# A deformable-convolution, attention and expert kernel: three gifts of the last batch go to two chunks, and the last finish starts with three head groups

## The chip, the cores and the metric

The kernel runs on one core of one Trainium2 chip. The metric is the device time of one execution in microseconds (us). PE is TensorE, DVE is VectorE, ACT is ScalarE, POOL is GpSimd, and SP is SyncE, which issues nearly all DMAs.

## The reference

The input `x` is a batch of 4 images, 128 channels of 64 x 64 positions. Everything is in fp32.

```
x = x + deform_conv3x3(group_norm(x))            # 9 taps, bilinear samples, offsets and mask from a 3x3 conv
t = tokens(x)                                     # [4, 4096, 128]
u = layer_norm(t)
q = ring(cos(heads(u) + rx))                      # 16 heads of 8
s = softmax(q @ q.T / sqrt(8))                    # per head, 4096 x 4096, queries = keys = values
x1 = layer_norm(u + (s @ q) @ w_comb.T + b)
t = t + layer_norm(x1 + w2 @ relu(w1 @ (cos(x1[:8]) * cos(ry))))
t = t + top2_of_8_experts(layer_norm(t))          # router softmax, 8 products 128x128, two weighted sums
```

The scores of a head are the product of one matrix with itself, so the block of scores of keys c and queries d is the transpose of the block of keys d and queries c.

## The kernel before

The 4096 tokens of an image are 8 chunks of 512. The 16 heads are 4 groups of 4 (`NGRP`). A **run** is one chunk of queries `sc` with one head group `g` of one batch `b`. It walks over key tiles of 128 tokens, 32 of them, and each is one **step**: `scores` (L1253 and after) makes four products of 128 x 512 on PE and two exponentials of 128 x 1024 on ACT (L1270, tile `e`), and `context` (L1274 and after) multiplies these with the values and a column of ones on PE into one accumulator `acc` (L1281). So `acc` holds the weighted sums of the four heads and, for each head, the sum of the weights. At the end of the run DVE copies `acc` into `cu` (L1493), and `park_context` stores it in DRAM (`atd`).

**Gifts.** A chunk that has computed the exponentials of keys t and its own queries can turn them: DVE transposes them in 32 x 32 blocks into `st` (`turn`, L1140), SP stores 1 MB in DRAM (`etd`). A later chunk that owns the tokens t as queries then fetches this tile (`fetch`, L1195, tile `et`) and needs no scores and no exponentials for it; its PE only multiplies it with the values of the giver (`from_turned`, L1214, 32 small products a tile, in two halves). `gifts` says to whom chunk `sc` gives: to `sc + 1`. So in batch 3 chunks 1 to 7 each take 4 tiles and compute 28 steps instead of 32 in each run. Two fetch buffers (`NET = 2`, counted by `room`) and three turning buffers (`NST = 3`) exist. The fetches are asked for 5 steps before the run that takes them; SP issues a fetch when a buffer is granted, and `returned` passes it on.

**Order.** In the last batch, batch 3, the runs go chunk by chunk, four head groups each. Nothing is scheduled by the chip: the program writes out the order of all instructions of PE, DVE, SP and POOL. Between the instructions of two steps `Beside` puts work of other jobs: the preparation of the next batch (none in batch 3) and the **finishes**. `finish(b, ch)` takes the four stored contexts of a chunk, divides by the sums of weights (a reciprocal of `rd`, a round trip through DRAM that spreads it to 128 partitions, and a product at L901), and then does `attention_out`, `feed_forward` and `experts` for the 512 tokens, one dependent step after the other. At most two finishes are in work at once (`active`); others wait in `done`.

`Beside` keeps a model of time: each step is `STEP = 1.82` us, and each gives PE `RATE = 0.44` us of credit for other work. A job yields `need(pe, dve, lat, ...)` before it emits; its instructions are put into the order only where the model has credit and the engine is free. Products with taken tiles are such a job too (`turned`), before all others, with `pe=MM256` (0.44) for each half of a tile; what is left of it at a run's last step is emitted at once. After the last step `beside.drain()` emits all that is left.

Each engine executes its instructions in the order written out, and waits on semaphores for the others. SP's DMA issues are in the same written order.

Of the kernel before, what the change touches and what calls it, by code (L numbers as in the profile page):

```python
# [224 lines left out]
def kernel(  # L225
# [669 lines left out]
    def attention_out(b, ch, r, aT, a4):  # L895
# [4 lines left out]
        yield need(dve=ve(512), lat=0.2)  # L900
        nc.vector.tensor_tensor(aT, aT, a4.rearrange("p i c -> p (i c)"), ALU.mult)  # L901
        for i in range(4):
# [74 lines left out]
    def experts(b, ch, x4):  # L977
# [75 lines left out]
        for i in range(4):  # L1053
            ws = [temp2(f"eo{b}_{ch}_{i}_{hf}") for hf in range(2)]
            for hf in range(2):
                for part in range(2):
                    yield need(pe=MM256, dve=ve(512) if part else 0.0, lat=FREE, hold=not part)
                    if part == 0:
                        pe = misc(f"e_ps{b}_{ch}_{i}_{hf}")
                    e0 = 4 * hf + 2 * part  # L1060
                    by_columns(
                        pe[:, 256 * part : 256 * (part + 1)], uT[:, P * i : P * (i + 1)],
                        ew_sb[:, e0 : e0 + 2, :].rearrange("p e c -> p (e c)"), True, True,
                    )
                nc.vector.tensor_tensor(  # L1065
                    ws[hf], pe.rearrange("p (e c) -> p e c", c=C),
                    gt[:, i, 4 * hf : 4 * (hf + 1), None].to_broadcast([P, 4, C]), ALU.mult,
                )
            yield need(dve=ve(512))
# [13 lines left out]

    def finish(b, ch):
        x4 = temp2(f"x4_{b}_{ch}")
        nc.sync.dma_start(out=x4, in_=x2d[b][ch])

        rows = atd[b][ch].rearrange("g (h d) n -> (g h) d n", d=32)
        aT = temp2(f"aT{b}_{ch}", (P, CH))
        nc.sync.dma_start(out=aT, in_=rows[:, :HD])  # L1090
        rd = work.tile([P, CH // HD], F32, tag="rd", name=f"rd{b}_{ch}")
        nc.sync.dma_start(out=rd, in_=rows[:, HD].rearrange("h (q n) -> h q n", q=HD))
        r = temp2(f"r{b}_{ch}")
# [4 lines left out]
        yield need(lat=3.5)  # L1098
        nc.sync.dma_start(out=rdd[b][ch].rearrange("h q n -> (h q) n"), in_=rd)
        yield need(lat=6.0)  # L1100
        a4 = temp2(f"a4_{b}_{ch}")
        nc.sync.dma_start(
            out=a4.rearrange("p i c -> p (i c)"),
            in_=rdd[b][ch].rearrange("h q n -> h (q n)")[:, None, :].to_broadcast([HEADS, HD, CH]),
        )
# [3 lines left out]


    def park_context(b, g, sc, cu):
# [50 lines left out]

    room = [NET]
    asking = []

    def granted(emit):
        if room[0]:
            room[0] -= 1
            emit()
        else:  # L1170
            asking.append(emit)

    def returned():
        if asking:
            asking.pop(0)()
        else:
            room[0] += 1

# [21 lines left out]

    def from_turned(run, acc):

        for giver in takes[run]:
            qv = values.pop((run, giver)).rearrange("p t x -> p (t x)")
            for kt in range(4):
                while (run, giver, kt) not in fetched:
                    yield need(lat=1.0)
                e, landed = fetched.pop((run, giver, kt))
                for half in range(2):
                    yield need(pe=MM256, hold=None, after=landed)  # L1210
                    for t in (2 * half, 2 * half + 1):
                        for h in range(4):
# [6 lines left out]
                            )  # L1219
                returned()  # L1220

# [188 lines left out]
    with tc.manual_schedule(engines={PE, DVE, SP, POOL}):  # L1410
# [6 lines left out]
        while n < len(steps):  # L1417
# [48 lines left out]
            if following:  # L1466
                if following[0] != b and at == 0:
                    beside.drain("prepare")

                if at == 1:  # L1470
# [3 lines left out]
                if takes[run + 1] and at == len(ts) - 5:  # L1474
                    fetch_values(run + 1)
                    for giver in takes[run + 1]:
                        for kt in range(4):
                            granted(lambda a=(run + 1, giver, kt): fetch(*a))
            by_act = run < opening
# [95 lines left out]
```

## Time and profile before

| | |
|---|---|
| median of 3 runs | 7592.69 us (7573.33 to 7599.12) |
| the profiled execution | 7579.71 us, its span 7576.5 us |
| PE, ACT, DVE busy, share of the span | 94%, 91%, 59% |
| bytes moved by DMA | 1689.51 MB, mean 223 GB/s |
| batch 3, from the end of batch 2's last run to the copy of the last accumulator | 5812.3 to 7493.0 us |
| after that | 83.5 us |

The profile is one execution. A busy time is the sum of an engine's instructions, and PE's is modelled, since matmuls overlap. What a wait costs is seen in the stretch where it stands: an engine that waits for one that is never idle sets nothing.

### The profile page before, as it was taken

How to read it: one execution, taken by the hardware profiler on the slowest of the kernel's cores; microseconds unless marked ns; L12 is line 12 of the kernel's file. 1: busy time of each engine (PE TensorE's matmuls, PEld its weight loads, DVE VectorE, ACT ScalarE, POOL GpSimd, SP SyncE). 2: the span in 40 equal slices, each digit the busy share in tenths (PEclk: the TensorE clock that was granted, in tenths of full speed). 3: DMA queues.
4: the chain of work that ended last, by engine and by line, in shares of the span. 5: the costliest groups of instructions: out<-in, count | busy, mean ns of one | idle time of the engine just before them, and what ended most of it. 6: DMA issues, size and time to landing. Idle time of an engine off the chain costs nothing.

```text
span 7576.5 us, 180754 instructions
## 1 busy us (share of the span) xinstructions
PE 7113.9 (94%) x73848; PEld 2375.9 (31%) x73848; DVE 4465.9 (59%) x8950; ACT 6863.5 (91%) x7467; POOL 1653.2 (22%) x1326
## 2 busy tenths in 40 slices
PE   3688999899999999999999999999999999999997
PEld 2122222223333333333333323333333333333333
DVE  7755356667444877776544677775444554455434
ACT  0578999889999999999999998989999999999995
POOL 5544034443000433422000334431000000000000
PEclk6889999999999999999999999999999999999998
DMA  6777567978446878887655789897454466666661
GB/s 181 223 204 219 141 223 241 300 234 291 149 168 200 292 244 280 268 277 244 203 179 190 228 279 298 289 324 237 174 190 152 148 236 230 232 222 239 226 202 63
DMA packets 909788, 1689.51 MB, mean 223 GB/s; under 512 B 150754, under 2 KB 384124, under 8 KB 858268
## 3 DMA queue, kind: packets, MB, share of 16 engines
q1 hardware_dynamic: 809102, 1371.37, 54.9%
q0 software_dynamic: 92160, 302.06, 12.4%
q8 instruction: 579, 9.49, 0.5%
q10 hardware_dynamic: 7694, 4.52, 0.2%
q14 instruction: 253, 2.07, 0.1%
HBM read 1027.51 MB, written 650.14 MB: 221 GB/s over the span
## 4 chain that ended last, share of the span: by engine, by line
PE 80%; DMA 8%; DVE 4%; issue 2%; ACT 2%; SPq 1%; another core or an unknown queue 0%; POOL 0%; POOLq 0%; DVEq 0%; ACTq 0%
PE acc L1281 39%; PE sc L1261 24%; PE acc L1214 5%; PE e_ps L281 4%; PE conv_ps L281 3%; DMA et<-etd 2%; PE f_ps L281 2%; ACT e L1270 2%; DMA etd<-st 1%; DMA sT<-smd 1%; PE om_ps L533 1%; DMA smd<-tr 1%; DVE st L1140 1%; DVE v L645 1%; DMA cu<-part 1%
## 5 line engine op out<-in xcount | busy, mean ns | idle before, releaser
L1270 ACT ACTIVATE e<-sc 128x1024 f32<-128x1024 f32 x7400 | 6849.4, 1081 | 527.0 <-PE sc L1261 368.1
L1281 PE MATMUL acc<-e,qf 128*9 128x512 f32 (+1 forms) x29600 | 3938.3, 601 | 18.6 <-ACT cu L1491 7.5
L1261 PE MATMUL sc<-qT,kT 32*128 32x512 f32 x14800 | 2368.7, 499 | 153.3 <-ACT e L1270 84.8
L1261 PEld LDWEIGHTS sc<-qT,kT 32*128 32x128 f32 x14800 | 942.8, 183 | 3612.6 <-ACT e L1270 3130.4
L625 POOL DMA_INDIRECT v<-tab,idx x1152 | 1451.8, 1260 | 1579.3 <-DVE tr L686 956.2
L1140 DVE STREAM_TRANSPOSE st<-e 128x1024 f32<-128x1024 f32 x792 | 937.3, 1222 | 752.4 <-ACT e L1270 620.1
L1281 PEld LDWEIGHTS acc<-e,qf 128*9 128x9 f32 (+1 forms) x29600 | 682.4, 91 | 610.3 <-issue 346.8
L396 POOL TENSOR_TENSOR r<-ln_t,expo 128x4 f32<-128x4 f32 x96 | 112.2, 1169 | 3105.4 <-DVE ln_t L394 3057.0
L645 DVE TENSOR_TENSOR v<-v,wt 128x1536 f32<-128x1536 f32 x384 | 667.0, 1737 | 119.5 <-DMA v<-tab,idx 96.8
L1214 PE MATMUL acc<-et,qv 128*9 128x128 f32 x12672 | 506.4, 276 | 52.2 <-DMA et<-etd 44.6
L1065 DVE TENSOR_TENSOR eo<-e_ps,gt 128x512 f32<-128x512 f32 x256 | 175.2, 686 | 552.5 <-PE e_ps L281 547.5
L650 DVE TENSOR_TENSOR v<-v 128x768 f32<-128x768 f32 x384 | 367.2, 956 | 10.1
L281 PE MATMUL conv_ps<-sT,wconv_sb 128*32 128x256 f32 x4320 | 351.0, 399 | 15.7 <-DMA sT<-smd 11.6
L1214 PEld LDWEIGHTS acc<-et,qv 128*9 128x9 f32 x12672 | 270.0, 90 | 254.4 <-issue 212.6
L686 DVE STREAM_TRANSPOSE tr<-v 128x128 f32<-128x128 f32 x1080 | 249.4, 282 | 37.5 <-DMA etd<-st 28.7
L1493 DVE COPY cu<-acc 128x512 f32<-128x512 f32 x116 | 80.2, 692 | 306.3 <-PE acc L1281 260.8
L651 DVE TENSOR_TENSOR v<-v 128x384 f32<-128x384 f32 x384 | 215.7, 562 | 13.3
L396 POOL TENSOR_TENSOR rstd<-lt_t,expo 128x4 f32<-128x4 f32 x32 | 57.9, 1811 | 575.9 <-DVE lt_t L394 550.7
L281 PE MATMUL f_ps<-w_sb,h 128*32 128x128 f32 x4096 | 166.1, 282 | 0.1
L950 DVE TENSOR_SCALAR h<-h_ps,b_sb 128x512 f32<-128x512 f32 x128 | 94.9, 744 | 100.3 <-PE h_ps L948 89.9
L823 POOL COPY fx<-rn 128x512 f32<-128x512 f32 x32 | 26.8, 838 | 526.3 <-DVE rn L822 321.4
L965 DVE TENSOR_TENSOR a<-a,f_ps 128x512 f32<-128x512 f32 x32 | 21.9, 685 | 198.8 <-PE f_ps L281 198.8
(227 smaller groups left out, 3166.9 us busy)
## 6 DMA issues: line engine op xcount, KB each, us to landing
etd<-st SPq DMA_DIRECT2D x396, 1024.0 KB
et<-etd SPq DMA_DIRECT2D x396, 1024.0 KB
kT<-kTd SPq DMA_DIRECT2D x372, 256.0 KB
smd<-tr SPq DMA_DIRECT2D x360, 192.0 KB
sT<-smd SPq DMA_DIRECT2D x360, 192.0 KB
qT<-qTd SPq DMA_DIRECT2D x166, 256.0 KB
atd<-cu SPq DMA_DIRECT2D x128, 256.0 KB
qf<-fqd SPq DMA_DIRECT2D x372, 72.0 KB
```

What stands on the lines that cost most here:

```text
L281: nc.tensor.matmul(dst[c : c + 32], lhsT=lhsT[:, c : c + 32], rhs=rhs, start=start, stop=stop)
L625: nc.gpsimd.indirect_dma_start(out=v[:, k, :], out_offset=None, in_=tab, in_offset=bass.IndirectOffsetOnAxis(ap=idx[:, j, kk : kk + 1], ax ...
L645: nc.vector.tensor_tensor(v4, v4, w12[:, :, None].to_broadcast([P, 12, C]), ALU.mult)
L650: nc.vector.tensor_tensor(v[:, :, : 2 * C], v[:, :, : 2 * C], v[:, :, 2 * C :], ALU.add)
L651: nc.vector.tensor_tensor(v[:, :, :C], v[:, :, :C], v[:, :, C : 2 * C], ALU.add)
L686: nc.vector.transpose(out=tr9[:, k, :, j % 4, :], in_=v[:, k, :C].rearrange("p (c i) -> p c i", i=32),)
L1065: nc.vector.tensor_tensor(ws[hf], pe.rearrange("p (e c) -> p e c", c=C), gt[:, i, 4 * hf : 4 * (hf + 1), None].to_broadcast([P, 4, C]), AL ...
L1140: nc.vector.transpose(out=st[:, :, 2 * pr : 2 * pr + 2, :].rearrange("p o h (q j) -> p o (h q) j", j=32), in_=es[pr].rearrange("p h (q o i ...
L1214: nc.tensor.matmul(acc[32 * h : 32 * h + QW, P * kt : P * (kt + 1)], lhsT=qv[:, at : at + QW], rhs=e[:, :, h, 32 * t : 32 * (t + 1)], star ...
L1261: nc.tensor.matmul(ps[i // 2][:, i % 2, :], lhsT=kT[h : h + 32, P * (t % 4) : P * (t % 4 + 1)], rhs=qT[h : h + 32, :], start=True, stop=True,)
L1270: nc.scalar.activation(e, ps[pr], AF.Exp, scale=1.0 / math.sqrt(HD))
L1281: nc.tensor.matmul(acc[32 * h : 32 * h + width, :], lhsT=flat[:, first : first + width], rhs=es[h // 2][:, h % 2, :], start=(t == ts[0]), ...
```

## The change

It has three parts, all in batch 3.

*Gifts.* Chunks 0, 2 and 4 give to the next two chunks. The next but one needs the tiles of keys in its own chunk, so in each run of chunks 0, 2 and 4 eight tiles are turned and stored, and chunks 2, 4 and 6 take eight tiles and compute 24 steps. For the fetches there are two more places, cut from the large tile `xs`, which the preparation of a batch uses and batch 3 no longer needs; the planner counts on these tiles 10 us after the fetch is emitted instead of 16.

*The last finish.* That of chunk 7 is a job of its own, `last`, of a rank ahead of the other finishes. It is added when three of its four groups are stored, loads and divides these 96 rows as before, and takes the fourth group's rows from `cu` in SBUF: two products with `picks` (made from the identity at the start) put the weighted sums and the sums of weights, each repeated 8 times, in rows 96 to 127 of two PSUM tiles, and a reciprocal and a product on DVE divide them. It waits until at most one other finish is in work. In its `experts`, the product with the gate and the sum are one fused operation for each expert, 32 in all, in place of products of 512 columns and a tree of sums.

*The end.* After the last step the planner goes on in steps of 0.3 us with more credit until no finish is left, and drains then.

```diff
+    by_head = ident.rearrange("p (h r) -> p h r", r=32)
+    picks = cpool.tile([P, 2, 4, HD], F32, name="picks")
+    nc.vector.tensor_copy(picks[:, 0], by_head[:, :, :HD])
+    nc.vector.tensor_copy(picks[:, 1], by_head[:, :, HD : HD + 1].to_broadcast([P, 4, HD]))
...
-        nc.vector.tensor_tensor(aT, aT, a4.rearrange("p i c -> p (i c)"), ALU.mult)
+        a = a4.rearrange("p i c -> p (i c)")
+        if (b, ch) == (NB - 1, NCH - 1):
+            nc.vector.tensor_tensor(aT[:96], aT[:96], a[:96], ALU.mult)
+            while not last_sums:
+                yield need(lat=1.0)
+            yield need(pe=1.7, dve=2 * ve(512), lat=0.2)
+            both = [misc(f"last_ps{k}") for k in range(2)]
+            for k in range(2):
+                nc.tensor.matmul(
+                    both[k][96:, :], lhsT=picks[:, k].rearrange("p h d -> p (h d)"),
+                    rhs=last_sums[0], start=True, stop=True,
+                )
+            nc.vector.reciprocal(a[96:], both[1][96:, :])
+            nc.vector.tensor_tensor(aT[96:], both[0][96:, :], a[96:], ALU.mult)
+        else:
+            nc.vector.tensor_tensor(aT, aT, a, ALU.mult)
...
+                if last:
+                    for e in range(4):
+                        nc.vector.scalar_tensor_tensor(
+                            x4[:, i, :], pe[:, C * e : C * (e + 1)],
+                            gt[:, i, 4 * hf + e : 4 * hf + e + 1], x4[:, i, :], ALU.mult, ALU.add,
+                        )
+                    continue
...
     def finish(b, ch):
+        ng = NGRP
+        if (b, ch) == (NB - 1, NCH - 1):
+            ng = NGRP - 1
+            while len(active) > 1:
+                yield need(lat=1.0)
...
     def park_context(b, g, sc, cu):
+        last = (b, sc) == (NB - 1, NCH - 1)
+        if last and g == NGRP - 1:
+            last_sums.append(cu)
+            return
 
         def put():
             nc.sync.dma_start(out=atd[b][sc][g], in_=cu)
             groups[b, sc] = groups.get((b, sc), 0) + 1
+            if last and groups[b, sc] == NGRP - 1:
+                beside.add("last", finish(b, sc), 0.7)
...
-    room = [NET]
+    room = [None] * NET
...
-    def fetch(run, giver, kt):
+    def fetch(run, giver, kt, place):
...
-        e = work.tile([P, 4, 4, P], F32, tag="et", name=f"et{run}_{giver}_{kt}", bufs=NET)
+        e = place
+        if e is None:
+            e = work.tile([P, 4, 4, P], F32, tag="et", name=f"et{run}_{giver}_{kt}", bufs=NET)
...
-        fetched[run, giver, kt] = e, beside.now + 16.0
+        fetched[run, giver, kt] = e, place, beside.now + (16.0 if place is None else 10.0)
...
     def gifts(b, g, sc):
         first = (4 if g == NGRP - 1 else 3) if b == 0 else 0
-        return [sc + 1] if first <= sc < NCH - 1 else []
+        if not first <= sc < NCH - 1:
+            return []
+        return [sc + 1, sc + 2] if b == NB - 1 and sc in (0, 2, 4) else [sc + 1]
...
+                if following[0] == NB - 1 != b and at == len(ts) - 6:
+                    spare_et = big.tile([P, KK, CH], F32, tag="xs", name="spare_et")
+                    spare_et = spare_et.rearrange("p k n -> p (k n)")
+                    for i in range(2):
+                        place = spare_et[:, 4 * CH * i : 4 * CH * (i + 1)]
+                        room.append(place.rearrange("p (r h x) -> p r h x", r=4, h=4))
...
         alone.append(True)
+        beside.STEP = 0.3
+        beside.rate = beside.RATE = 4.0
+        beside.fills = 8
+        while beside.has("finish") or beside.has("last"):
+            beside.step(0.8)
         beside.drain()
```

More of the change, by code (lines that the diff above doesn't have):

```diff
@@ L1053, in experts @@
         for i in range(4):
-            ws = [temp2(f"eo{b}_{ch}_{i}_{hf}") for hf in range(2)]
+            last = (b, ch) == (NB - 1, NCH - 1)
+            ws = [] if last else [temp2(f"eo{b}_{ch}_{i}_{hf}") for hf in range(2)]
             for hf in range(2):
@@ L1068, in experts @@
                 )
+            if last:
+                continue
             yield need(dve=ve(512))
@@ L1084, in finish @@
     def finish(b, ch):
+        ng = NGRP
[3 more added lines that the diff above has]
+                yield need(lat=1.0)
         x4 = temp2(f"x4_{b}_{ch}")
         nc.sync.dma_start(out=x4, in_=x2d[b][ch])
-        rows = atd[b][ch].rearrange("g (h d) n -> (g h) d n", d=32)
+        rows = atd[b][ch][:ng].rearrange("g (h d) n -> (g h) d n", d=32)
         aT = temp2(f"aT{b}_{ch}", (P, CH))
-        nc.sync.dma_start(out=aT, in_=rows[:, :HD])
+        nc.sync.dma_start(out=aT[: 32 * ng], in_=rows[:, :HD])
         rd = work.tile([P, CH // HD], F32, tag="rd", name=f"rd{b}_{ch}")
+        rd = rd[: 32 * ng]
         nc.sync.dma_start(out=rd, in_=rows[:, HD].rearrange("h (q n) -> h q n", q=HD))
@@ L1098, in finish @@
         yield need(lat=3.5)
-        nc.sync.dma_start(out=rdd[b][ch].rearrange("h q n -> (h q) n"), in_=rd)
+        back = rdd[b][ch][: 4 * ng]
+        nc.sync.dma_start(out=back.rearrange("h q n -> (h q) n"), in_=rd)
         yield need(lat=6.0)
@@ L1102, in finish @@
         nc.sync.dma_start(
-            out=a4.rearrange("p i c -> p (i c)"),
-            in_=rdd[b][ch].rearrange("h q n -> h (q n)")[:, None, :].to_broadcast([HEADS, HD, CH]),
+            out=a4.rearrange("p i c -> p (i c)")[: 32 * ng],
+            in_=back.rearrange("h q n -> h (q n)")[:, None, :].to_broadcast([4 * ng, HD, CH]),
         )
@@ L1108, in finish @@
         yield from experts(b, ch, x4)
+    last_sums = []
     def park_context(b, g, sc, cu):
+        last = (b, sc) == (NB - 1, NCH - 1)
+        if last and g == NGRP - 1:
+            last_sums.append(cu)
+            return
         def put():
@@ L1161, in etd_slot, with returned @@
         return etd[key]
-    room = [NET]
+    room = [None] * NET
     asking = []
     def granted(emit):
-        if room[0]:
-            room[0] -= 1
-            emit()
+        if room:
+            emit(room.pop(0))
         else:
             asking.append(emit)
-    def returned():
+    def returned(place):
         if asking:
-            asking.pop(0)()
+            asking.pop(0)(place)
         else:
-            room[0] += 1
+            room.append(place)
     def fetch_values(run):
@@ L1207, in from_turned @@
                     yield need(lat=1.0)
-                e, landed = fetched.pop((run, giver, kt))
+                e, place, landed = fetched.pop((run, giver, kt))
                 for half in range(2):
@@ L1219, in from_turned @@
                             )
-                returned()
+                returned(place)
     keys, queries, values = {}, {}, {}
@@ L1477 @@
                         for kt in range(4):
-                            granted(lambda a=(run + 1, giver, kt): fetch(*a))
+                            granted(lambda place, a=(run + 1, giver, kt): fetch(*a, place))
             by_act = run < opening
```

## The prediction

> **What bounds the kernel now.** I read the page first, then the busy time by chunk of batch 3 (the only batch whose order the change moves), then the waits, then the tail.
>
> ```profile
> PE 7113.9 (94%) x73848; PEld 2375.9 (31%) x73848; DVE 4465.9 (59%) x8950; ACT 6863.5 (91%) x7467; POOL 1653.2 (22%) x1326
> L1270 ACT ACTIVATE e<-sc 128x1024 f32<-128x1024 f32 x7400 | 6849.4, 1081 | 527.0 <-PE sc L1261 368.1
> L1140 DVE STREAM_TRANSPOSE st<-e 128x1024 f32<-128x1024 f32 x792 | 937.3, 1222 | 752.4 <-ACT e L1270 620.1
> ```
>
> PE and ACT look equally full, so the mean can't say which one sets the pace. The stretches of chunks 0, 1, 3 and 7 of batch 3 and the waits can:
>
> ```profile
> 5812.30:6047.60 235.30, 235.22 (x2280) 75.28 (x2280) 134.63 (x322) 235.28 (x259) 7.05 (x7) 1.00 0.47 154
> 6047.60:6254.00 206.40, 206.18 (x2387) 72.07 (x2387) 105.57 (x232) 206.33 (x227) 5.34 (x5) 1.00 0.68 232
> 6461.10:6667.40 206.30, 205.84 (x2357) 71.65 (x2357) 107.61 (x252) 206.12 (x226) 6.04 (x6) 1.00 0.68 235
> 7288.10:7493.00 204.90, 204.59 (x2332) 71.84 (x2336) 61.32 (x190) 203.64 (x223) 5.34 (x5) 1.00 0.39 127
> ...
> PEld sc L1261 <- ACT e L1270: 688.4, 890, 0.9
> ```
>
> Columns: stretch, length, busy PE, PEld, DVE, ACT, POOL, clock, DMA share, GB/s. ACT is never idle, and PE's longest wait is for ACT. Chunk 0 has 4 runs of 32 steps, the others 4 of 28: 235.3/128 = 206.4/112 = 1.84 us a step, two exponentials. A step not computed is worth 1.84 us, if nothing else becomes late.
>
> The tail, from the copy of the last accumulator:
>
> ```profile
> 7493.03 0.69 DVE L1493 COPY cu<-acc 128x512 f32<-128x512 f32 x1
> ...
> 7504.54 0.54 DVE L1097 RECIPROCAL rd<-rd 128x64 f32<-128x64 f32 x1
> ...
> 7510.16 0.69 DVE L901 TENSOR_TENSOR aT<-aT,a 128x512 f32<-128x512 f32 x1 [4.54 <-DMA a<-rdd]
> ...
> 7493.00:7511.00 18.00, 6.54 (x101) 4.05 (x93) 11.97 (x23) 0.00 (x0) 0.00 (x0) 0.73 0.29 92
> 7511.00:7576.50 65.50, 26.72 (x325) 16.12 (x325) 39.38 (x121) 0.23 (x1) 3.02 (x3) 0.60 0.01 5
> ```
>
> 82.8 us follow the copy's end (7493.7): what is left of finish (3,6), the round trip of the last chunk's sums, then 65.5 us of one serial chain.
>
> **Part 1, the gifts.** 3 more gifts x 4 groups x 4 tiles = 48 steps fewer: 48 x 1.84 = -88 us. Added are 48 tiles turned (96 DVE transposes x 1.22 us, beside other work while DVE is half idle), 48 stores and 48 fetches of 1.05 MB, and on PE 32 small matmuls a tile. These lie in two halves in successive steps, and the rows of the last run show such a step still 1.84 us long. So the engines carry it; what may not is DMA. Chunks 2 and 4 now give 8 tiles and take 8 in each run of 24 steps. A 4-and-4 chunk moves 232 GB/s x 206.4 us = 47.9 MB; with 16 more stores and 16 more fetches, and 4 key loads of 0.34 MB fewer, it is 80 MB, in 96 x 1.84 = 177 us of ACT time: 450 GB/s. What DMA can do is seen in two runs of batch 2 and one short stretch:
>
> ```profile
> 4544.10:4603.30 59.20, 55.45 (x660) 20.07 (x656) 44.97 (x70) 52.43 (x58) 31.25 (x25) 1.00 1.05 350
> 4958.90:5017.10 58.20, 54.51 (x614) 18.39 (x610) 41.80 (x58) 52.47 (x57) 27.54 (x23) 1.00 1.03 367
> 4930.00:4940.00 10.00, 9.74 (x126) 3.59 (x124) 8.43 (x16) 8.26 (x9) 5.01 (x5) 1.00 1.04 408
> ```
>
> At share 1.03 to 1.05 it is full, and gives 350 to 367 GB/s over a run (408 for 10 us). 80 MB then take 218 to 229 us. Four fetch places (4.2 MB) and three turning buffers (3.1 MB) let some 20 us run in the neighbouring chunks: 198 to 209 us, a stall of 21 to 32 a chunk; I take 27. Bounds: 0 at 408 GB/s, 52 at 350 without the overlap. The stall falls on PE (a take waits for its fetch; behind it on PE stand scores and contexts, and so ACT) and on DVE (a transpose waits for its buffer; e is released late, and ACT stops). SP is in order too: fetches into a returned place wait there for PE, with stores and key loads behind them. Chunk 6 takes 8 and gives 4: 63 MB, 173 to 181 us against 177: 3 us (0 to 5). Together +57 us (0 to 110). More places and the earlier "landed" estimate cost nothing by themselves; the memory they use was last written for batch 2.
>
> The Trainium skill, "DMA: Bandwidth & Descriptors", Specifications and Bandwidth, speaks for the gifts: a fabric ceiling of 435 GB/s and 425 measured on one core for 16 MB. By it 80 MB would take an estimated 188 us, less the overlap: no stall, and this term would be 0. The rows of batch 2 show no run near it, and I go by them.
>
> **Part 2, what the gifts do to the finishes.** This decides. Finishes get on PE only the planner's credit: 0.44 us a step, from which each taken tile is charged 0.88. 48 steps fewer lose 21 us of credit and 48 tiles more eat 42: 63 us. The view of the order per engine shows the result. Before, behind the last context matmul PE has 6 groups of expert products of (3,6), and then the last chunk. After, it has there: (3,4) from its transposed u on, nearly all of (3,5), all of (3,6), and only then the first product of the last chunk. On DVE 293 instructions stand between the copy of the last accumulator and the reciprocal of the last sums: 49 of (3,4), about 120 each of (3,5) and (3,6). With the durations of the same lines before, they are 104.1 us (a whole finish from L901 on: 122 instructions, 42.7 us; so 2.44 finishes). Both queues are in order: none of this can run earlier. Gaps of 0.03 us between DVE instructions (starts 0.22 apart, 0.19 long) add 9: 113 us at least. The lone chain of the tail has DVE busy for 39.4 of 65.5 us; at that share it would be 173. Here two finishes alternate, so most waits are covered: I take 130.
>
> **Part 3, the last finish.** It was to start three groups early, but its DVE and PE work stands behind those finishes, so only the round trip (7504.5 to 7510.2) is saved. In its place: two products, hidden among the (3,6) work; a reciprocal of 32x512 from PSUM (not seen; 128x4 takes 0.18 and 128x64 0.55, so 6 ns an element, 3.3 us; bounds 0.55, as for 64 elements, and 3.3); a product, 0.7. Then the chain of 65.5 us, +0.7 for the copy of y of (3,6) that now stands in it, and -1.5 for the expert sums: 32 fused operations at 0.32 to 0.37 us (near L1075's 0.29 and L788's 0.34, with the gap; -1.9 to 0) for 4 x 3.03. Together 69 us (66 to 70). The store of the fourth group's context (256 KB) goes; two copies for `picks` at the start lie in DVE's wait for x (3.85 us). Tail: 130 + 69 = 199 for 82.8: +116 us (+96 to +160).
>
> **Sum.** The profiled execution took 7579.7 us (span 7576.5 and 3.2 around it). -88 + 57 + 116 = +85: 7665. The median of the runs shown is 13 us above it: 7678.
>
> **Rivals.**
> - Same tail, but DMA keeps up (408 GB/s, and its share of 0.68 in a 4-and-4 chunk leaves room for a while): -88 + 116 = +28, 7621. Against it: 450 GB/s are asked for over 177 us, and no row shows that.
> - DMA hurts more: without any overlap each way, +110, and a slower tail of +130: +152, 7745. For it: each wait stands in an in-order queue, so one late fetch holds everything.
> - The other side, faster: the finishes keep pace, and the tail shrinks as the change says, by the round trip and a little more (-12); with the same DMA stall -88 + 57 - 12 = -43, 7550. It decides only if DVE's queue ahead of the last copy holds (3,4) to (3,6); the order says it doesn't. If the order misleads, this is the case.
>
> **Chances.** Forecast (around +85) 0.62, DMA keeps up 0.20, worse 0.13, faster 0.03; 0.02 for none of these. About 0.3% (23 us) is what can be told from no change here. Faster by more: 0.03. Within: 0.07, the low end of the second case (its tail at +96 gives +8). Slower: 0.90. The range reaches from +8 (the second case with the short tail) to +157 (just past the third): 7601 to 7750.
>
> **What would show it.** Steps at 1.84 us in chunks 0, 1, 3, 5, 7; chunks 2 and 4 near 204 us (not 177) with DMA share near 1; chunk 6 near 180; last accumulator copied some 31 us earlier (near 7462); 199 us after it, of which some 130 until the 32x512 reciprocal. I am wrong in part 1 if chunks 2 and 4 take 177 us with share below 1, in part 2 if the first product of the last chunk comes within 30 us of the copy.

## The result, and the profile after

| | before | after |
|---|---|---|
| median | 7593.91 us (4 runs, 7573.33 to 7599.12) | 7638.98 us (4 runs, 7634.9 to 7643.02) |
| ratio, 95% interval | | 1.0069 [1.0055, 1.0084] |
| the profiled execution, its span | 7579.71, 7576.5 us | 7643.02, 7641.2 us |
| batch 3 up to the copy of the last accumulator | 1680.7 us | 1628.4 us (-52.3) |
| from the end of that copy to the end | 82.8 us | 194.2 us (+111.4) |

The change makes the kernel 45 us slower by the medians: it was forecast at +85, with a range from +8 to +157. From profile to profile the span grew by 64.7 us. The two stages of batch 3 make 59.1 of that. The other 5.6 lie ahead of batch 3, where the order of instructions is the same but for the two small copies that make `picks`; the profile of before is one of the quicker of its kernel (14 us under its median), and that of after the slowest of its four. The interval of the ratio is 42 to 64 us, so it holds the 45 of the medians and the 59 of the stages alike. Each step is judged by the stages of the profiles, and the whole by the medians.

The page of after, the lines of engines and of the two groups that the gifts change. The line numbers moved: L1270 is now L1315, L1140 is L1184, L1493 is L1546.

```profile
PE 7111.3 (93%) x74812; PEld 2408.7 (32%) x74812; DVE 4574.4 (60%) x9058; ACT 6782.0 (89%) x7371; POOL 1662.2 (22%) x1326
...
L1315 ACT ACTIVATE e<-sc 128x1024 f32<-128x1024 f32 x7304 | 6767.3, 1079 | 560.2 <-PE sc L1306 367.8
...
L1184 DVE STREAM_TRANSPOSE st<-e 128x1024 f32<-128x1024 f32 x888 | 1050.9, 1222 | 907.4 <-ACT e L1315 681.9
```

The gifts did what they say: 96 exponentials fewer (7304 for 7400), 96 transposes more (888 for 792), at the same durations. ACT is busy for 81.5 us less, DVE for 108.5 more. PE's busy time, which is modelled, is the same as before: as far as it can be read, a gift takes work from ACT and none from PE.

The busy time of after by stretch: chunks 1, 2, 4, 6 and 7 of batch 3, then the tail up to the reciprocal of the last sums and from there on (stretch, length, busy PE, PEld, DVE, ACT, POOL with their instructions, clock, DMA share, GB/s).

```profile
6053.20:6260.00 206.80, 206.80 (x2427) 72.63 (x2427) 104.10 (x223) 206.66 (x227) 4.03 (x4) 1.00 0.66 229
6260.00:6451.70 191.70, 184.74 (x2368) 70.67 (x2366) 113.77 (x209) 178.91 (x196) 5.03 (x5) 0.99 1.02 393
...
6658.40:6856.60 198.20, 185.44 (x2422) 70.28 (x2422) 104.15 (x137) 179.05 (x194) 1.01 (x1) 0.97 1.03 389
...
7063.80:7241.00 177.20, 177.03 (x2464) 68.29 (x2460) 69.33 (x123) 177.20 (x193) 3.02 (x3) 1.00 0.96 351
7241.00:7446.30 205.30, 205.11 (x2363) 71.73 (x2364) 71.59 (x211) 204.02 (x223) 5.03 (x5) 1.00 0.41 135
7447.00:7571.40 124.40, 65.72 (x787) 38.42 (x787) 96.33 (x294) 0.69 (x3) 6.65 (x6) 0.70 0.07 22
7571.40:7641.20 69.80, 30.61 (x345) 17.84 (x345) 45.49 (x137) 0.23 (x1) 3.02 (x3) 0.60 0.02 8
```

Chunks 1 and 7 stand at 1.84 us a step (112 steps), and so do 3 (206.7), 5 (207.2) and 0 (235.3 for 128 steps). Chunk 6 takes eight tiles and gives four: 177.2 us, 96 steps at 1.85. Chunks 2 and 4 have 96 steps too and should take 176.6; they take 15.1 and 21.6 us more, at a full DMA share and with ACT idle for 13 and 19 us. Chunks 2, 4 and 6 won 54.0 us against before, and the five others lost 1.7. Then 1132 PE instructions stand behind the last copy where before there were 426, and 431 on DVE where there were 144.

The beginning of both parts of the tail on DVE:

```profile
7446.28 0.69 DVE L1546 COPY cu<-acc 128x512 f32<-128x512 f32 x1 [1.30 <-PE acc L1326]
...
7571.40 3.36 DVE L917 RECIPROCAL a<-last_ps 32x512 f32<-32x512 f32 x1
```

The last sums lie ready in SBUF at 7447, and 124.4 us pass until they are used. Nothing that the last chunk needs is late: DVE executes the finishes (3,4), (3,5) and (3,6), which stand ahead of it in its queue.

What waited in chunks 2 to 4 of after (engine, tile and line, whom for; us in total, times, the longest):

```profile
DVE st L1184 <- DMA etd<-st: 96.2, 29, 6.8
...
ACT e L1315 <- DVE st L1184: 20.1, 13, 9.1
...
DVE rd L1132 <- DMA rd<-atd: 17.2, 2, 13.8
...
ACT e L1315 <- PE acc L1326: 6.2, 6, 1.2
...
PEld acc L1259 <- DMA spare_et<-etd: 1.4, 4, 0.6
```

The full DMA shows on DVE, which waits 96 us in 29 waits for a turning buffer whose store has not left; ACT then waits 20.1 us for DVE to release `e`, and 6.2 for PE's context products. PE waits 1.4 us for a fetched tile. One wait is of another kind: at 6819.6 DVE had stood for 13.8 us before the reciprocal of `rd`, a small load of a finish behind fetches on SP, and ACT's 9.1 us follow at 6821.9.

### The profile page after: what moved, and what is told of

Read it like the earlier page. It is cut to its first block, busy times and chain, and to the rows that moved or that the text cites. A ratio compares the mean times of both kernels' runs of the same rounds, so it can differ in the third digit from the quotient of the medians.

```text
span 7641.2 us, 182763 instructions
## 1 busy us (share of the span) xinstructions
PE 7111.3 (93%) x74812; PEld 2408.7 (32%) x74812; DVE 4574.4 (60%) x9058; ACT 6782.0 (89%) x7371; POOL 1662.2 (22%) x1326
## 4 chain that ended last, share of the span: by engine, by line
PE 79%; DMA 9%; DVE 5%; issue 2%; ACT 2%; SPq 1%; POOL 1%; another core or an unknown queue 1%; ACTq 0%; POOLq 0%; DVEq 0%
PE acc L1326 37%; PE sc L1306 23%; PE acc L1259 6%; PE conv_ps L281 3%; PE e_ps L281 3%; DMA et<-etd 2%; PE f_ps L281 2%; ACT e L1315 2%; DMA etd<-st 2%; DMA sT<-smd 1%; PE om_ps L537 1%; DVE v L649 1%; DVE st L1184 1%; DMA kT<-kTd 1%; DMA cu<-part 1%
## 5 line engine op out<-in xcount | busy, mean ns | idle before, releaser
L1315 ACT ACTIVATE e<-sc 128x1024 f32<-128x1024 f32 x7304 | 6767.3, 1079 | 560.2 <-PE sc L1306 367.8
L1326 PE MATMUL acc<-e,qf 128*9 128x512 f32 (+1 forms) x29216 | 3887.6, 601 | 18.5 <-DVE cu L1546 8.4
L1306 PE MATMUL sc<-qT,kT 32*128 32x512 f32 x14608 | 2333.1, 500 | 177.7 <-ACT e L1315 108.5
L1306 PEld LDWEIGHTS sc<-qT,kT 32*128 32x128 f32 x14608 | 927.4, 183 | 3591.5 <-ACT e L1315 3087.6
L1184 DVE STREAM_TRANSPOSE st<-e 128x1024 f32<-128x1024 f32 x888 | 1050.9, 1222 | 907.4 <-ACT e L1315 681.9
L1259 PE MATMUL acc<-et,qv 128*9 128x128 f32 x11648 | 468.9, 277 | 54.8 <-DMA et<-etd 45.3
L1259 PEld LDWEIGHTS acc<-et,qv 128*9 128x9 f32 x11648 | 249.1, 90 | 243.6 <-issue 201.3
L1546 DVE COPY cu<-acc 128x512 f32<-128x512 f32 x116 | 80.2, 692 | 313.9 <-PE acc L1326 272.1
```

The source lines that it names most:

```text
L1184: nc.vector.transpose(out=st[:, :, 2 * pr : 2 * pr + 2, :].rearrange("p o h (q j) -> p o (h q) j", j=32), in_=es[pr].rearrange("p h (q o i ...
L1259: nc.tensor.matmul(acc[32 * h : 32 * h + QW, P * kt : P * (kt + 1)], lhsT=qv[:, at : at + QW], rhs=e[:, :, h, 32 * t : 32 * (t + 1)], star ...
L1306: nc.tensor.matmul(ps[i // 2][:, i % 2, :], lhsT=kT[h : h + 32, P * (t % 4) : P * (t % 4 + 1)], rhs=qT[h : h + 32, :], start=True, stop=True,)
L1315: nc.scalar.activation(e, ps[pr], AF.Exp, scale=1.0 / math.sqrt(HD))
L1326: nc.tensor.matmul(acc[32 * h : 32 * h + width, :], lhsT=flat[:, first : first + width], rhs=es[h // 2][:, h % 2, :], start=(t == ts[0]), ...
```

## The experiments

All start from the kernel after, except where one is named. **Attention** is batch 3 up to the copy of the last accumulator, and the **tail** is what follows the end of that copy. Chips differ ahead of batch 3, so a ratio is to runs of the kernel before on the same chip, and the rest goes by stages.

| run | batch 3 to the last copy | tail | time, us |
|---|---|---|---|
| before | 1680.7 | 82.8 | 7593.91 |
| after | 1628.4 | 194.2 | 7638.98; ratio 1.0069 [1.0055, 1.0084] |
| one_gift | 1692.1 | 72.4 | 7464.69; 0.9996 [0.9987, 1.0006] |
| gifts_alone | 1630.6 | 234.5 | 7564.52; 1.0130 [1.0113, 1.0147] |
| two_fills | 1702.3 | 69.9 | 7472.25; 1.0005 [0.9996, 1.0015] |
| half_stores | 1600.1 | 194.2 | 7482.32, one run; before 7463.52 |
| two_places | 1680.9 | 74.5 | 7573.84; 0.9989 [0.9978, 1.0000] |
| extra_loads | 1643.9 | 193.0 | 7665.46, one run; before 7582.33 |
| fills_one_gift | 1743.1 | 70.4 | 7630.15, one run; before 7582.33 |
| later_finish | 1632.1 | 216.0 | 7669.52, one run; before 7582.33 |
| gift_of_4 | 1678.7 | 107.1 | 7595.8; 1.0021 [1.0009, 1.0034] |
| gift_of_0 | 1663.6 | 128.9 | 7600.6, one run; before 7578.87 |
| wide_takers | 1652.8 | 121.9 | 7587.65, one run; before 7578.87 |
| gift_of_4_later | 1655.5 | 114.5 | 7474.94, one run; before 7472.92, one run |

Where the code is untouched the stages repeat: the tail of half_stores is 194.2, that of extra_loads 193.0. And where both kernels have many runs on one chip, the sum of the two stages against before agrees with the medians within 6 us: +1.0 and +1.2 us in one_gift, +8.7 and +8.7 in two_fills, -8.1 and -8.5 in two_places, +22.3 and +16.9 in gift_of_4. So the stages' 59 is at least as good a figure for the change as the medians' 45.

**one_gift.** The finish and the end of the change, without its gifts.

```diff
-        return [sc + 1, sc + 2] if b == NB - 1 and sc in (0, 2, 4) else [sc + 1]
+        return [sc + 1]
```

> The change without its extra gifts: every chunk of batch 3 gives to the next chunk alone; the last finish from SBUF, the fused expert sums and the interleaved end stay. My theory (the gifts push two and a half finishes behind the attention, nothing else makes the tail long): attention in batch 3 takes 1681 us as before (28 steps of 1.84 us), 12 DVE instructions of (3,6) are left behind it, and the tail is 82.8 - 9 (round trip) - 1.5 (expert sums) = some 72 us: 10 us faster than before, 7583. Rival (the long tail comes from the new form of the last finish, its waiting for the other finish and the interleaved end): the tail stays near 194 us and the kernel is some 110 us slower than before.

The tail fell to 72.4 us, 10.4 under before: the last finish does what it was written for once nothing stands ahead of it. So the +111 of after come from the gifts. But the attention took 11 us more than before, 4 of them in chunk 4 (211.9) and 4 in chunk 7 (209.1), so that the kernel is level with before and not 10 us faster. A place of this is in the waits of the stretch from 6558 to 6574, and in DVE's timeline there:

```profile
DVE aT L920 <- DMA a<-rdd: 7.4, 1, 7.4
ACT e L1315 <- PE sc L1306: 5.5, 1, 5.5
PEld ao_ps L281 <- DVE x L1071: 4.4, 1, 4.4
```

```profile
6566.65 0.69 DVE L920 TENSOR_TENSOR aT<-aT,a 128x512 f32<-128x512 f32 x1 [7.39 <-DMA a<-rdd]
```

DVE stands 7.4 us before a product of a finish, whose divisors are still on their way; PE in its order waits for DVE, and ACT for PE. With four places four fetches of 1 MB leave at once, and the small transfer is behind them, as SP's timeline from 6520 to 6575 shows:

```profile
6549.53 1.16 SPq L1240 DMA_DIRECT2D et<-etd  x2
6550.73 1.42 SPq L1240 DMA_DIRECT2D spare_et<-etd  x2
...
6555.49 0.93 SPq L1138 DMA_DIRECT2D a<-rdd  x1
```

**gifts_alone.** The gifts and their places, with the last finish and the end as before.

```diff
-        if (b, ch) == (NB - 1, NCH - 1):
+        if False:
...
-            last = (b, ch) == (NB - 1, NCH - 1)
+            last = False
...
-        if (b, ch) == (NB - 1, NCH - 1):
+        if False:
...
-        last = (b, sc) == (NB - 1, NCH - 1)
+        last = False
...
-        beside.STEP = 0.3
-        beside.rate = beside.RATE = 4.0
-        beside.fills = 8
-        while beside.has("finish") or beside.has("last"):
-            beside.step(0.8)
```

> The extra gifts and the two fetch places alone; the last finish waits for all four groups as before, and the end is drained one job after the other. My theory: attention 1628 us as in the changed kernel, 421 DVE instructions behind it, less well alternated than in the changed kernel: a tail of 200 to 250 us, so 10 to 50 us slower than the changed kernel, 7650 to 7690. Rival (gifts are nearly free, the rest of the change costs): 30 to 50 us faster than before.

The tail of gifts_alone, by the busy time:

```profile
7320.00:7554.50 234.50, 93.85 (x1128) 55.55 (x1128) 141.39 (x421) 0.92 (x4) 9.06 (x9) 0.62 0.06 17
```

DVE is busy for 141.4 us, as in the tail of after (96.3 + 45.5 = 141.8), but spread over 40 us more. Its share is 0.60, that of the lone chain of before (39.4 of 65.5); in after it is 0.77 up to the reciprocal. So the forecast's upper bound of 173 us, "at that share", is what the old end does, and what kept after below it is the new end and the early start. How the 40 us divide between these two was not run apart.

**two_fills.** All parts of the change, and room for the finishes: a step may hold two pieces of other work, at more credit.

```diff
-                    fills and self.fills == 1 and self.credit - job["need"][0] < -self.LATE
+                    fills and self.fills < 3 and self.credit - job["need"][0] < -self.LATE
...
-            beside.fills = 3 if run < 12 else 1
+            beside.fills = 3 if run < 12 else 2 if b == NB - 1 else 1
...
+                    beside.rate = beside.RATE = 0.6
```

> The whole change, but in batch 3 the planner may put two pieces of other PE work in a step instead of one, with 0.60 us of credit a step instead of 0.44. In the written order all of (3,4), (3,5) and (3,6) now stand before the last context product. My theory: the tail is 7 + 65 = some 74 us (194 in the changed kernel); attention gets longer by at most the PE time of 2.44 finishes (23 us each, 56 us), of which the waits for DMA in chunks 2 and 4 hide half: 1628 + 25. Together some 35 us faster than before (7557), 80 faster than the changed kernel. Rival (PE is full in batch 3, so that what is put beside costs what it costs behind): attention 1628 + 110, no gain over the changed kernel.

The tail fell to 69.9 us: the finishes had kept pace, as the faster rival asked. I had expected that to be worth 35 us in all, and it came out even, since the attention grew by 74 us over after, not by 25. The busy time of the whole attention, and the wait that is new in it (before has 0.3 us of it):

```profile
5689.80:7392.10 1702.30, 1682.11 (x19801) 610.15 (x19801) 932.65 (x1990) 1613.19 (x1738) 39.58 (x39) 0.99 0.74 262
```

```profile
ACT e L1315 <- PE sc L1306: 66.1, 173, 5.2
```

ACT waited 173 times for scores, 0.4 us each. Chunks 3 and 5, which have no extra tile, grew by 8.6 and 8.3 us. The credit is not what binds: with the credit raised to 0.6 alone PE's order as written out is that of after, instruction for instruction (that kernel was not run). What binds is the one piece that a step may hold, which the taken tiles have first.

**half_stores.** In chunks 2 and 4 the tiles for the next chunk are turned and not stored, so that the next chunk multiplies what lay there before. 16 of 32 stores a chunk are gone.

```diff
+            if b == NB - 1 and sc in (2, 4) and t // 4 == sc + 1:
+                turning.discard((g, sc, t))
+                return
```

> The whole change, but chunks 2 and 4 leave out the stores of the tiles that they give to the next chunk (16 of 1.05 MB in each); the taker fetches what an earlier chunk left there. The turning on DVE, the fetches and all PE work stay. If DMA bandwidth stalls chunks 2 and 4 (75 and 77 MB at 390 GB/s): 59 MB need 151 us, and both chunks fall from 192 and 198 to the ACT time, 177 us. Rival (DVE's turning or PE's products with taken tiles stall them): they stay at 192 and 198.

Chunks 2 and 4 of half_stores:

```profile
6127.70:6305.70 178.00, 177.46 (x2370) 67.89 (x2370) 113.76 (x210) 177.62 (x196) 5.04 (x5) 1.00 0.96 339
6511.90:6696.00 184.10, 179.48 (x2424) 67.54 (x2420) 104.20 (x136) 178.17 (x194) 1.01 (x1) 0.99 0.96 340
```

178.0 us: with 339 GB/s moved, chunk 2 is near its pace. The same instructions on PE, DVE and ACT (but for 2 on PE and 1 on DVE) cost 13.7 us more with the stores. So the stall comes with the stores. Whether by their bytes or by the turning buffers that they hold, this run can't tell, since a tile that isn't stored leaves its buffer free at once; the next run can. Chunk 4, at the same rate, keeps 6 us. They stand behind a finish's small load, as its waits from 6512 to 6696 show:

```profile
DVE rd L1132 <- DMA rd<-atd: 9.4, 1, 9.4
ACT e L1318 <- DVE st L1184: 4.7, 1, 4.7
```

DVE's wait ends at 6659.7, its transposes follow, and ACT's wait for them ends at 6662.1; ACT's only other wait in the chunk is of 1.0 us.

**extra_loads.** The other way: chunk 6, at its pace in after, gets five idle loads of 0.79 MB a run.

```diff
+            if b == NB - 1 and sc == 6 and at % 5 == 2:
+                idle_v = work.tile([P, 3, 4 * C], F32, tag="v", name=f"idle{run}_{at}", bufs=NV)
+                nc.sync.dma_start(
+                    out=idle_v.rearrange("p k q -> p (k q)"),
+                    in_=tabs[0][: 6 * P].rearrange("(p k) c -> p (k c)", k=6),
+                )
```

> The whole change, and in each run of chunk 6 five loads of 0.79 MB from DRAM into an SBUF buffer that nothing uses (15.7 MB in the chunk; no engine but the issuing SP does more). Chunk 6 takes 8 tiles and gives 4, and goes at ACT's pace in the changed kernel (177 us at 351 GB/s). If bandwidth makes the stalls of chunks 2 and 4: 62 + 16 = 78 MB at 390 GB/s are 200 us, and chunk 6 comes to 190 to 200 us, with DMA share above 1. Rival (the three turning buffers stall them, whatever else DMA does): 8 gifts in a run are not there, chunk 6 stays at 177.

```profile
7073.40:7264.80 191.40, 181.11 (x2464) 69.32 (x2464) 69.43 (x124) 177.84 (x193) 3.02 (x3) 0.98 1.04 392
```

That is chunk 6 of extra_loads: 14.2 us longer than in after, at 392 GB/s, the same rate as in chunks 2 and 4. In after it moved 62.2 MB (351 GB/s x 177.2 us); with 20 loads of 0.79 MB that would be 78, and 75 of them moved within the chunk. A third chunk that is asked for more stops at the same rate, with four tiles to turn in a run and not eight. So the bytes alone make a stall. But it sits elsewhere, since DVE has no wait for a turning buffer here: PE waits for fetched tiles, and ACT for PE (11.5 us in 3).

```profile
PE acc L1259 <- DMA spare_et<-etd: 8.6, 3, 3.1
```

**two_places.** one_gift without the two more places for fetches, that is, the last finish and the end alone.

```diff
-                if following[0] == NB - 1 != b and at == len(ts) - 6:
-                    spare_et = big.tile([P, KK, CH], F32, tag="xs", name="spare_et")
-                    spare_et = spare_et.rearrange("p k n -> p (k n)")
-                    for i in range(2):
-                        place = spare_et[:, 4 * CH * i : 4 * CH * (i + 1)]
-                        room.append(place.rearrange("p (r h x) -> p r h x", r=4, h=4))
```

> One gift each as in one_gift, and the two fetch places and the estimate of 16 us of the kernel before: what is left of the change is the last finish, the fused sums and the interleaved end. one_gift's attention lost 8 us where DVE waited in order for a finish's own small transfer (7.4 and 4.5 us, with ACT idle 5.5 and 2.9 us behind it). My theory: that transfer was late because four places let four fetches of 1 MB be issued at once; with two places attention is 1681 us again, tail 72: 10 us faster than before (ratio 0.9987). Rival (the places have nothing to do with it, the new rank and order of the finishes makes the wait): attention stays near 1692 and the kernel is level with before.

The attention and the tail of two_places:

```profile
5817.80:7498.70 1680.90, 1678.57 (x18749) 578.43 (x18753) 817.41 (x1876) 1678.07 (x1834) 39.92 (x39) 1.00 0.61 208
7499.40:7573.90 74.50, 35.21 (x417) 20.11 (x413) 51.68 (x150) 0.23 (x1) 3.02 (x3) 0.69 0.02 8
```

The attention is that of before again (1680.9 for 1680.7): one_gift's 11 us were the places, with the estimate of 10 us that goes with them. The longest wait for divisors (`aT` for `a`) is 2.1 us here and 7.4 in one_gift. The tail is 8.3 us shorter than before, and the ratio 0.9989 [0.9978, 1.0000] on 11 runs says the same 8 us. This is the fastest of all versions; it lies within the 0.3% that I called no change.

**fills_one_gift.** two_places with the three edits of two_fills, to see whether two_fills' 74 us are PE's total work (then nothing here, since there are no extra tiles) or its unevenness (two pieces in one step make that step late, and the next doesn't give it back).

```diff
+                    fills and self.fills < 3 and self.credit - job["need"][0] < -self.LATE
...
+            beside.fills = 3 if run < 12 else 2 if b == NB - 1 else 1
...
+                    beside.rate = beside.RATE = 0.60
```

> As two_places, with the two pieces a step and 0.60 us of credit of two_fills. Nearly the same finishing work lies in attention as in two_places (0.4 of a finish more). two_fills' attention was 74 us longer than the changed kernel's for 2.44 finishes, 30 us each. If that is the price of PE time in a full PE: attention 1681 + 0.4 x 30, some 1690. If two pieces in one step cost by their unevenness (a step of 2.3 us, which later steps can't give back): 1730 or more.

The attention of fills_one_gift, and ACT's wait for scores in it:

```profile
5813.10:7556.20 1743.10, 1738.57 (x18841) 598.98 (x18837) 825.66 (x1895) 1694.44 (x1834) 40.22 (x39) 1.00 0.59 201
```

```profile
ACT e L1315 <- PE sc L1306: 44.9, 136, 2.7
```

92 PE instructions more than two_places (0.5%) and 62 us more, 4 us of them given back in the tail. So the extra tiles aren't the cause, and unevenness, which asked for 1730 us or more, stands; it is argued from the length here, and not shown step by step. Of the 62 us ACT is idle for 46 more, and its busy time grew by 16 at the same 1834 instructions. PE's busy time grew by 60 us on 92 instructions: it grows with the length, and is no measure of PE's work here.

**later_finish.** A theory for the rest of the stall: finishes wait for small transfers behind bursts of fetches. Here the planner leaves more time before it uses them.

```diff
-        yield need(lat=4.0)
+        yield need(lat=16.0 if b == NB - 1 and ch < NCH - 1 else 4.0)
...
+        if b == NB - 1 and ch < NCH - 1:
+            yield need(lat=12.0)
```

> The whole change, but in batch 3 the planner counts 16 us instead of 4 for the loads at a finish's start, and 12 us more for the spread reciprocals. In the changed kernel's chunk 4 DVE waited 13.9 us in order for such a load, and ACT 9.1 us behind it. My theory: part of chunk 4's stall is that wait and not the large transfers: chunk 4 falls from 198 to some 189, chunk 2 stays near 192; the tail grows by a few us, since the finishes start later still. Rival (the time is lost to bandwidth in any case): chunk 4 stays at 198.

Chunks 2 and 4 took 191.0 and 201.6 us; I had expected chunk 4 at 189. The largest of DVE's waits in its chunks 2 to 4 (the lines stand two lower):

```profile
DVE st L1186 <- DMA etd<-st: 131.9, 37, 7.6
```

The finishes' waits that the edit aimed at went (that for `rd` from 17.2 us to 3.8), and DVE then waited 36 us more for its turning buffers. The theory fell: where DMA is full, a wait removed ahead of it only lets DVE reach the full queue sooner. And the later finishes made the tail 22 us longer.

**gift_of_4** and **gift_of_0.** Only one of the three gifts, to price one alone.

```diff
-        return [sc + 1, sc + 2] if b == NB - 1 and sc in (0, 2, 4) else [sc + 1]
+        return [sc + 1, sc + 2] if b == NB - 1 and sc == 4 else [sc + 1]
```

(gift_of_0 has `sc in (0,)`.)

> The whole change with one extra gift in place of three: chunk 4 alone gives to two (chunk 6 takes 8 and gives 4, which went at ACT's pace). No chunk asks DMA for more than 360 GB/s. In the written order 66 DVE instructions (29 us, 32 with gaps) of the finishes before stand between the last copy and the reciprocal; in the changed kernel 293 (105 us, 115 with gaps) took 124. My theory (the gift saves its 16 steps in full, 29 us, and pays them back behind the attention): attention 1652 (up to 8 more if a finish's transfer is late), tail 70 + 34 = 104; sum 1756, before 1763.5: within 10 us of before, no gain from the gift over two_places (1755). Rival (the waits for DMA in chunks 2 and 4 are what spoils the change, and a gift without them pays): 20 to 30 us faster than two_places, 30 to 40 faster than before.

> The same with chunk 0 as the one that gives to two (chunk 2 takes 8 and gives 4). The saved steps are the same 16, but five chunks follow in which the planner could make up for the finishes that are put off. In the written order 125 DVE instructions (45 us, 50 with gaps) stand before the reciprocal, more than for chunk 4, since every step's place for other work is taken all the way to the end. My theory: attention 1652, tail 70 + 54 = 124; sum 1776, 12 us slower than before in batch 3 and the tail. Rival (an early gift is made good by the end): tail below 90.

The tails came as expected, 107.1 and 128.9 us: one gift alone sends 33 to 54 us behind the last copy (74.5 in two_places), for 29 us (16 x 1.84) of ACT time. The gift of chunk 0 costs more than that of chunk 4; why was not tested. The attention missed, by 27 us (8 of which I had allowed for) and by 12. In gift_of_4 the taker is at its pace (chunk 6, 177.4), and chunks 4 and 5 lost 10 each (217.3 and 217.0); in gift_of_0 chunk 3 lost them (216.2). The waits of gift_of_4's attention:

```profile
DVE aT L920 <- DMA a<-rdd: 23.7, 7, 7.9
...
ACT e L1315 <- PE sc L1306: 18.9, 8, 8.0
DVE rd L1132 <- DMA rd<-atd: 16.7, 4, 7.1
```

This is one_gift's mechanism with more of it: 11 waits of DVE for a finish's small transfers, and 8 of ACT behind them.

**wide_takers.** Two pieces a step in chunks 2, 4 and 6 alone, where ACT waits for DMA anyway in two of them.

```diff
-                    fills and self.fills == 1 and self.credit - job["need"][0] < -self.LATE
+                    fills and self.fills < 3 and self.credit - job["need"][0] < -self.LATE
...
+            if b == NB - 1:
+                wide = sc in (2, 4, 6)
+                beside.fills = 2 if wide else 1
+                beside.rate = beside.RATE = 0.6 if wide else 0.44
```

> The whole change, with two pieces of other PE work in a step and 0.60 us of credit in chunks 2, 4 and 6 alone, which take 8 tiles; one piece and 0.44 elsewhere. 116 DVE instructions (45 us, 49 with gaps) are left behind instead of 293. My theory: in chunks 2 and 4 PE's work hides in the waits for DMA, which were 15 and 22 us there, and in chunk 6, which has none, it shows: chunks 2 and 4 longer by under 4 us each, chunk 6 by about 10 (188 in two_fills); attention 1628 + 16, tail 70 + 53 = 123: sum 1767, level with before and 55 faster than the changed kernel. Rival (the pieces cost the same wherever they stand): chunks 2 and 4 longer by 11 each as in two_fills (203.9 and 208.8).

The tail is 121.9 us, 72 less than after. Chunks 2 and 4 grew by 0.4 and 3.3 us (192.1 and 201.5): the finish work there went into the DMA stall. Chunk 6, which has no stall, grew by 15.2, where I had expected 10, and chunk 3 by 7.0. In sum -48 us against after, 11 more than before.

**gift_of_4_later.** gift_of_4, with 14 and 10 us left for the finishes' transfers, as in later_finish.

```diff
-        yield need(lat=4.0)
+        yield need(lat=14.0 if b == NB - 1 and ch < NCH - 1 else 4.0)
...
+        if b == NB - 1 and ch < NCH - 1:
+            yield need(lat=10.0)
...
-        return [sc + 1, sc + 2] if b == NB - 1 and sc in (0, 2, 4) else [sc + 1]
+        return [sc + 1, sc + 2] if b == NB - 1 and sc == 4 else [sc + 1]
```

> gift_of_4, with 14 us instead of 4 counted for the loads at a finish's start in batch 3 and 10 us more for the spread reciprocals. gift_of_4's attention took 1678.7 us where 1652 were expected; ACT was idle in eight places (18.9 us, the longest 8.0), and DVE waited 23.7 and 16.7 us for a finish's own small transfers. My theory (four fetches of 1 MB issued at once delay those transfers; DVE, in order, holds up PE and ACT): the waits go, attention is 1652; 92 DVE instructions (38 us with gaps) are left behind, tail 70 + 41 = 111; sum 1763, level with before (1763.5) and 8 us slower than two_places (1755). Rival (the transfers are not the cause, or the time is lost to bandwidth anyway, as in later_finish): attention stays near 1679.

Its attention took 1655.5 us, 25.4 less than two_places and near the 29 of 16 steps. The waits:

```profile
ACT e L1317 <- PE sc L1308: 2.0, 3, 1.4
...
DVE aT L920 <- DMA a<-rdd: 1.3, 1, 1.3
```

gift_of_4's 23.7 and 18.9 us have gone, and this time nothing took their place; no chunk here is full on DMA. The tail is 114.5 us, so that one gift without any stall still loses: -25.4 + 40.0 = +14.6 us against two_places.

## Why the prediction was right, point by point

**The steps.** Chunks 0, 1, 3, 5 and 7 stayed at 1.84 us a step and chunk 6 came at 177.2 for the expected 180. The -88 us are there.

**The DMA stall was the mis-sized term.** I gave it 57 us; it is 15.1 + 21.6 + 0.6 = 37. That the bytes make it is shown from both sides, by half_stores and extra_loads. The failing step is the rate: "At share 1.03 to 1.05 it is full, and gives 350 to 367 GB/s over a run". Chunks of whole tiles kept 389 to 393 GB/s for 190 us and more. The runs of batch 2 had gathers beside the tiles (POOL is busy for 31 and 28 us there); that these made them slower was not tested. A second term was off the other way: of my 80 MB, 75 to 77 moved within the chunk, so 3 to 5 lay outside it, where I had let 7.3 MB or 20 us run in the neighbours. With the measured rate and my overlap the stall would be 80 MB / 391 GB/s = 205, less 20, against 177: 8 us, and half_stores puts the stores' share at 14. The two errors pull against each other: that my 57 lies only 20 above the 37 is in part luck. The 408 GB/s of a 10 us stretch was the nearer row: 76 MB at it give 186 us. The Trainium skill, "DMA: Bandwidth & Descriptors", Specifications and Bandwidth, has 425 GB/s measured for one core; no run here reaches it over a chunk (393 at most). The same page's limit of about 358 GB/s for HBM per core, which is half of what two cores share, is exceeded by all three full chunks. The measurement stands between the two.

**Where the stall sits** was half wrong: I named PE's takes first and DVE's turning buffers second. PE waited 1.4 us for fetches, DVE 96 us for buffers. In chunk 4 a part of the stall in after stands behind a finish's load, but later_finish shows that it can't be had by moving that wait. That more places and the earlier "landed" estimate "cost nothing by themselves" was wrong too: one_gift and two_places put them at 11 us of attention with one gift each. What they cost in the whole change was not run apart.

**The deferral** was right in size and in place: 124.4 us until the reciprocal for the 130 taken, 294 DVE instructions for the 293 counted, tail 194.2 for 199. It came from the order as written out, and not from the model that I gave beside it. "Finishes get on PE only the planner's credit" names the wrong limit: what the extra tiles take is the one place a step has (two_fills). Had the credit been the limit, more of it would have mended this. The last copy came 46.7 us earlier than before where I had 31, with a batch that began 5.6 us later: the stall again.

**The last finish.** 69.8 us from the reciprocal on, for 69; the reciprocal 3.36 for 3.3. The fused sums were to save 1.5 us and saved none. The group of these, in the answer for their line:

```profile
L1087 DVE SCALAR_TENSOR_TENSOR x<-e_ps,gt,x x32: 341/351/352, 7624.4 to 7636.3; 128x128 f32<-128x128 f32 x32
```

The first starts at 7624.4 and the last ends at 7636.65: 12.2 us, for four times 3.03.

**The rivals.** "DMA keeps up" would have 177 us in chunks 2 and 4, which only chunk 2 of half_stores comes near (178.0). The faster side needed the finishes to keep pace; two_fills made them, and the longer attention took the gain. The -12 that this case gave the tail came as -10.4 in one_gift and -12.9 in two_fills. The sum of the terms as measured: -88 + 37 + 111, and 60 for the forecast's 85. Of these 25 us 20 are the DMA term and 5 the tail. The profiles' stages give 59.1, the medians 45, and the interval of 42 to 64 holds both. By the medians alone the result is nearer to the +28 of "DMA keeps up" than to +85; that it isn't that case is told by the stalls of chunks 2 and 4, and not by the sum.

## What to carry to other kernels

A step removed from the engine that sets the pace is worth its time only if the other work that used that step's place has another one: here one gift freed 25 to 29 us and sent 33 to 54 us of finish work to the end, where nothing lies beside it. Read that from the order of the in-order queues, not from a budget: count the instructions ahead of the last one that matters, and add up their durations from the profile. And before moving bytes into a stretch, take the rate from a stretch with the same mix of transfers. A burst of large transfers also holds up the small one behind it, and with it the engine that waits for it (7.4 us in one_gift).

## What the runs showed of the hardware

Stores and fetches of 1 MB tiles together (in one chunk with loads of 0.79 MB beside them) went at 389 to 393 GB/s for 191 to 198 us, in three chunks of two kernels. Two pieces of work in one step where a step of the attention has room for one cost 62 us over a batch for 92 more PE instructions, though ACT's single waits for it are 0.3 us each (44.9 us in 136). And with four fetches out at once, DVE's longest wait for a finish's divisors was 7.4 us (one_gift) and 7.9 (gift_of_4), against 2.1 with two (two_places). Its longest for the small load `rd` was 13.8 us in after, where DMA was full besides, against 6.7 in two_places.
